# Cross-attention of a Perceiver layer: turns and products of one group issued between the steps of the next, reciprocal deviations turned by transposes

## The chip, the cores and the metric

The kernel runs on one core of one Trainium2 chip. The time is device microseconds from launch to end; three runs of the kernel before gave 571.45, 571.56 and 575.35 us, median 571.56 us. All arithmetic is in float32.

## What is computed

One layer: cross-attention of 32 x 32 queries on a context of 257 rows per batch entry, then self-attention with 16 heads, then a mixture of eight experts of which each token takes two. The change lies in the cross-attention alone:

```
def _L0_xattn_ref(modality1, modality2, ln1_g, ln1_b, ln2_g, ln2_b, Wq, bq, Wk, bk, Wv, bv, Wo, bo):
    x1 = layernorm(modality1, ln1_g, ln1_b)
    x2 = layernorm(modality2, ln2_g, ln2_b)
    q = x1 @ Wq + bq
    k = x2 @ Wk + bk
    v = x2 @ Wv + bv
    scores = jnp.einsum('bqe,bke->bqk', q, k) * scaling
    attn = jax.nn.softmax(scores, axis=-1)
    ctx = jnp.einsum('bqk,bke->bqe', attn, v)
    return ctx @ Wo + bo
...
x = x + _L0_xattn_ref(_layernorm(x, axis=-1), ctx_768, ...)
x = x + _L0_attn_ref(_layernorm(x, axis=-1), ...)
x = x + _L0_ffn_ref(_layernorm(x, axis=-1), ...)
```

x is (32, 32, 512), the context (32, 257, 384), every projection has 512 outputs.

## The kernel before

The 32 batch entries are taken in eight **groups** of four; a group has 4 x 32 = 128 query rows, one per partition. Two groups make a **pair**. Key and value projections are not carried out on the context: the kernel folds Wq with Wk (tile mq) and Wv with Wo (tile wvo) once, so that a group needs only products with the raw context, and the layernorm of the context comes in as one reciprocal standard deviation per context row.

For group g these steps exist, each a function:

- `cstats(g)` (L498): nine statistics instructions on VectorE over the context tile n and its last row nl, a few small ones, and on GpSimd the power -1/2 (L519), which gives rs, one number per context row, with context rows on the partitions. Its statistics are held behind an instruction in the table `pace`: those of group g+2 behind the instruction that makes u of group g (L597, L601).
- `rspread(g)` (L522): ScalarE repeats rs into rx (L526; one buffer only), four blocks of 32 equal columns, and copies the last row's number (L532).
- `xscores(g)` (L535): TensorE multiplies the queries q2T by the transposed context nT into pscore (L542). TensorE then turns rx into prs (L551) by an ordinary product with the identity, so that the deviations lie along the free dimension, and ScalarE copies it to rb (L555). VectorE multiplies pscore by rb and takes the row maximum (L558, then L565 and L567), ScalarE takes the exponential (L571), VectorE multiplies by rb again (L574): the tile ex.
- `xmix(g)` (L579): TensorE turns ex (two transposes into pte, L584), ScalarE copies it to eT (L586), TensorE multiplies eT by n into pc (L590), VectorE adds the last row and makes u (L597). It also issues the loads of group g+3, on SyncE's queue, and at g = 4 those of the four self-attention weights and the zero fill of a DRAM list.
- `xout(g)` (L611): TensorE turns u (three transposes into ptu, L615), ScalarE copies to uT (L617), TensorE multiplies by wvo into po (L620), VectorE adds to x_sb (L623).

For a pair p there are `xnorm(p)` (statistics of x and the normalised y), `xturn(p)` (eight transposes of y, L446, evacuated by ScalarE to x1T), `xquery(p)` (the queries: 36 products counted as instructions, L475, L467, L484) and `xbias(p)` (VectorE adds). `norm(0)`, `turn(0)` (L365), `project(0, j, half)` (L380, j = 0 for q and 1 for k) and `rotate(0, j)` (L396 to L409) belong to the self-attention stage and are already placed here for its first pair.

The loop (L726) writes, for each g: xscores(g), cstats(g+1), rspread(g+1), xout(g-1), then xturn or xquery of the next pair or a piece of the self-attention, and last xmix(g). The turn and its product stand side by side in xmix and in xout: on TensorE, pte, a wait for ScalarE's copy, pc; ptu, a wait for ScalarE's copy, po.

The program text is not the order on the engines. A scheduler of the framework lays out each engine's instructions before the run, keeps the text's order as priority, and by its own estimates of time lets later instructions go ahead of one that it takes to be waiting. On the engine the order is then fixed. PSUM tiles come from two pools of four buffers: `ps` (pscore, pc, po, pq, pb, pp, spt) and `ps2` (pte, prs, ptu, pt).

Of the kernel before, what the change touches and what calls it, by code (L numbers as in the profile page):

```python
# [28 lines left out]
NTT = 8  # L29
# [22 lines left out]
def tile_perceiver_layer(  # L52
# [22 lines left out]
    nc = tc.nc  # L75
# [16 lines left out]
    ident = cpool.tile([P, P], F32, name="ident")  # L92
# [132 lines left out]
    with ExitStack() as attn:  # L225
# [19 lines left out]
        with ExitStack() as xa:  # L245
# [246 lines left out]
            def xbias(p):  # L492
                for i in range(2):
                    nc.vector.tensor_add(
                        x_sb[:, 2 * p + i, :], x_sb[:, 2 * p + i, :], xrow
                    )

            def cstats(g):  # L498

                n, nl = gs[g]["n"], gs[g]["nl"]  # L500
                st = spool.tile([P, 9, 6], F32, tag="st9", bufs=2, name="st9")

                with tc.issue_after(pace["c", g]):
                    for r in range(9):
                        nc.vector.bn_stats(  # L505
                            st[:, r, :], n[:, r // 2, r % 2, :] if r < 8 else nl
                        )

                d = spool.tile([P, 9], F32, tag="d9", bufs=2, name="d9")
                nc.vector.tensor_tensor(d, st[:, :, 1], st[:, :, 4], ALU.subtract)  # L510
                nc.vector.scalar_tensor_tensor(
                    d, d, DC / 4.0, d, op0=ALU.mult, op1=ALU.mult
                )
                v = spool.tile([P, 9], F32, tag="v9", bufs=2, name="v9")
                nc.vector.tensor_tensor(v, st[:, :, 2], st[:, :, 5], ALU.add)
                nc.vector.tensor_tensor(v, v, d, ALU.add)
                nc.vector.tensor_scalar(v, v, 1.0 / DC, EPS, ALU.mult, ALU.add)  # L517
                rs = spool.tile([P, 9], F32, tag="rs9", bufs=2, name="rs9")
                nc.gpsimd.tensor_tensor(rs, v, mhalf[:, :9], ALU.pow)  # L519
                gs[g]["rs"] = rs  # L520
# [13 lines left out]

            def xscores(g):  # L535
                p, i = g // 2, g % 2
                q2T, qb, nT, rb = qs[p]["q2T"], qs[p]["qb"], gs[g]["nT"], gs[g]["rb"]
                pscore = ps.tile([P, D], F32, tag="ps", name="pscore")
                for c in range(KC):
                    for b in range(4):  # L540
                        o = i * P + b * T
                        nc.tensor.matmul(  # L542
                            pscore[ts(b, T), 0:S],
                            q2T[:, c, o : o + T],
                            nT[:, c, b, :],
                            start=(c == 0), stop=(c == KC - 1),
                        )

                pr = ps2.tile([P, 2, P], F32, tag="pt", name="prs")
                for c in range(2):  # L550
                    nc.tensor.matmul(  # L551
                        pr[:, c, :], gs[g]["rx"][:, c].rearrange("p b q -> p (b q)"),
                        ident, start=True, stop=True,
                    )
                nc.scalar.copy(rb[:, 0:NK], pr.rearrange("p c k -> p (c k)"))  # L555
                ex = wk.tile([P, S], F32, tag="ex", name="ex")
                mx = spool.tile([P, 1], F32, tag="mx", name="mx")
                top = nc.vector.tensor_tensor_reduce(  # L558
                    out=ex, in0=pscore[:, 0:S], in1=rb, scale=1.0, scalar=-3.0e38,
                    op0=ALU.mult, op1=ALU.max, accum_out=mx,  # L560
                )
                if g % 2 or g == 0:
                    pace["x", p + 1 + g % 2] = top.ins
                mq_ = spool.tile([P, 1], F32, tag="mq", name="mxq")
                nc.vector.tensor_tensor(mq_, mx, qb[:, i : i + 1], ALU.add)  # L565
                nm = spool.tile([P, 1], F32, tag="nm", name="nm")
                nc.vector.tensor_scalar(  # L567
                    nm, qb[:, i : i + 1], mq_, XSCALE, ALU.subtract, ALU.mult
                )
                sm = spool.tile([P, 1], F32, tag="sm", name="sm")  # L570
                gs[g]["exp"] = nc.scalar.activation(  # L571
                    ex, ex, AF.Exp, bias=nm, scale=XSCALE, accum_out=sm
                ).ins
                nc.vector.tensor_tensor(ex, ex, rb, ALU.mult)  # L574
                rc = spool.tile([P, 1], F32, tag="rc", name="rc")
                nc.vector.reciprocal(rc, sm)
                gs[g]["ex"], gs[g]["rc"] = ex, rc

            def xmix(g):  # L579

                n, nl, ex = gs[g]["n"], gs[g]["nl"], gs[g]["ex"]
                pt = ps2.tile([P, 2, P], F32, tag="pt", name="pte")
                for c in range(2):
                    nc.tensor.transpose(pt[:, c, :], ex[:, ts(c, P)], ident)  # L584
                eT = wk.tile([P, 2, P], F32, tag="eT", name="eT")
                nc.scalar.copy(eT, pt)  # L586
                pc = ps.tile([P, D], F32, tag="ps", name="pc")
                for c in range(2):
                    for b in range(4):
                        nc.tensor.matmul(  # L590
                            pc[ts(b, T), 0:DC],
                            eT[:, c, ts(b, T)],
                            n[:, b, c, :],
                            start=(c == 0), stop=(c == 1),
                        )
                u = wk.tile([P, DC], F32, tag="u", name="u")
                mixed = nc.vector.scalar_tensor_tensor(  # L597
                    u, nl, ex[:, NK : NK + 1], pc[:, 0:DC], op0=ALU.mult, op1=ALU.add
                )
                gs[g]["u"] = u  # L600
                pace["c", g + 2] = mixed.ins  # L601
                if g + 3 < NTT:
                    gs[g + 3] = load_ctx(g + 3)
                    if g + 4 == NTT:

                        with tc.issue_after(gs[g + 3]["last"]):
                            for n, s in zip("qkvo", (aWqT, aWkT, aWvT, aWoT)):
                                aw[n] = load_weight(s, weight_room("a" + n))
                        fill(aw["last"])

            def xout(g):  # L611
                u = gs[g]["u"]
                pt = ps2.tile([P, KC, P], F32, tag="pt", name="ptu")
                for c in range(KC):
                    nc.tensor.transpose(pt[:, c, :], u[:, ts(c, P)], ident)  # L615
                uT = wk.tile([P, KC, P], F32, tag="uT", name="uT")
                nc.scalar.copy(uT, pt)  # L617
                po = ps.tile([P, D], F32, tag="ps", name="po")
                for c in range(KC):
                    nc.tensor.matmul(  # L620
                        po, uT[:, c, :], wvo[:, c, :], start=(c == 0), stop=(c == KC - 1)
                    )
                nc.vector.scalar_tensor_tensor(  # L623
                    x_sb[:, g, :], po, gs[g]["rc"], x_sb[:, g, :],
                    op0=ALU.mult, op1=ALU.add,
                )
# [96 lines left out]
                nc.tensor.matmul(pm, firsts, part, start=True, stop=True)  # L723
                nc.vector.tensor_add(xrow, pm, row[:, RBO : RBO + D])

            for g in range(NTT):  # L726
                p = g // 2
                xscores(g)
                if g + 1 < NTT:
                    cstats(g + 1)  # L730
                    rspread(g + 1)
                if g == 0:
                    fold_values()
                    xbias(0)
                else:
                    xout(g - 1)
                if p + 1 < NTT // 2:
                    if g % 2 == 0:
                        if g == 0:
                            xnorm(1)  # L740
                        xturn(p + 1)
                        xbias(p + 1)
                    else:
                        xquery(p + 1)
                        if p + 2 < NTT // 2:
                            xnorm(p + 2)

                if g == NTT - 3:
                    norm(0)
                elif g == NTT - 2:  # L750
                    turn(0)
                elif g == NTT - 1:
                    project(0, 0, 1)
                    rotate(0, 0)
                xmix(g)
                if g >= NTT - 2:
                    project(0, g - (NTT - 2), 0)
            xout(NTT - 1)
            project(0, 1, 1)
            rotate(0, 1)  # L760

        av, ao = aw["v"], aw["o"]
# [776 lines left out]
```

## Time and profile before

| what | value |
|---|---|
| median of three runs | 571.56 us |
| the profiled execution, device time | 572.78 us |
| its span, first to last instruction | 571.0 us |
| mean granted TensorE clock | 0.975 |
| TensorE busy | 529.5 us (93%) |
| VectorE busy | 254.1 us (44%) |
| ScalarE busy | 123.5 us (22%) |
| GpSimd busy | 83.3 us (15%) |

The cross-attention's loop takes the stretch from 30.7 us (first pscore) to 146.6 us. Its groups start their score products (L542) at 30.67, 48.63, 63.51, 71.90, 87.70, 96.09, 111.31 and 123.37 us. In the lists of waits below, a line says which engine's instruction (tile and line) waited for which, then the microseconds in total, the number of waits, and the longest. In the timeline, a line has the start and the length in us, the engine, the line of the code, the operation, output <- inputs, the count, and in brackets the idle time before it with what ended it.

### The profile page before, as it was taken

Reading aid. Unit: us, or ns where it says so; the run is one execution under the profiler, and the core shown is the slowest. Engines: PE = TensorE matmul, PEld = TensorE weight load, DVE = VectorE, ACT = ScalarE, POOL = GpSimd, SP = SyncE. Lnnn points to the kernel's source line nnn. Section 1 sums busy time; section 2 is a strip of 40 time slices with the busy share of each in tenths; the row PEclk is TensorE's granted clock in tenths of the full one; section 3 lists DMA queues with packets and bytes.
Section 4 is the critical chain, followed back from the end, with each engine's and each line's share of the span. In section 5 each row is a group of like instructions: output and inputs, shape, how many; then the busy total and the mean of one; then the engine's idle time right before and its main releaser. Section 6 shows DMA issues by size and latency. Waiting matters only on the chain.

```text
span 571.0 us, 11331 instructions
## 1 busy us (share of the span) xinstructions
PE 529.5 (93%) x4732; PEld 344.2 (60%) x4732; DVE 254.1 (44%) x758; ACT 123.5 (22%) x274; POOL 83.3 (15%) x120
## 2 busy tenths in 40 slices
PE   6999887998999999998988999999999999999992
PEld 3655454655675685785647546556657475777580
DVE  6657688554677675577535122112213131222120
ACT  3533434231321412312113011001102020111010
POOL 2110231110000004004212110012120211112111
PEclk9999999999999989889889999999999999999997
DMA  7999967999920002002086323566553554746421
GB/s 275 382 366 381 350 215 260 361 385 386 386 95 38 2 3 113 4 2 115 34 332 265 116 42 137 188 178 212 160 137 111 161 199 153 210 161 194 158 26 21
DMA packets 43086, 104.51 MB, mean 183 GB/s; under 512 B 3985, under 2 KB 7185, under 8 KB 42002
## 3 DMA queue, kind: packets, MB, share of 16 engines
q1 hardware_dynamic: 38434, 94.91, 46.1%
q0 software_dynamic: 4592, 8.78, 7.4%
q8 instruction: 39, 0.64, 0.4%
q14 instruction: 21, 0.17, 0.1%
HBM read 75.50 MB, written 28.18 MB: 182 GB/s over the span
## 4 chain that ended last, share of the span: by engine, by line
PE 69%; DVE 2%; issue 1%; ACT 1%; POOL 0%; POOLq 0%; ACTq 0%
PE ph L1319 17%; PE fpo L1372 15%; PE pp L380 9%; PE ppv L793 5%; PE ppo L869 4%; PE fpq L1286 4%; PE phe L1123 2%; PE poe L1137 2%; PE pg L915 2%; PE pos L850 2%; PE pqs L808 2%; PE phb L1340 1%; PE xpt L1301 1%; ACT xT L176 1%; PE fpt L906 1%
## 5 line engine op out<-in xcount | busy, mean ns | idle before, releaser
L1319 PE MATMUL ph<-xT,w 128*128 128x288 f32 (+4 forms) x448 | 100.2, 382 | 3.1 <-ACT xT L176 3.1
L1319 PEld LDWEIGHTS ph<-xT,w 128*128 128x128 f32 x448 | 79.0, 190 | 19.6 <-ACT xT L176 3.7
L1372 PE MATMUL fpo<-w,hT 128*128 128x512 f32 x192 | 84.4, 596 | 0.0
L1372 PEld LDWEIGHTS fpo<-w,hT 128*128 128x128 f32 x192 | 35.9, 190 | 43.9 <-issue 43.7
L1325 DVE TENSOR_TENSOR hT<-ph,sg 128x288 f32<-128x288 f32 (+4 forms) x56 | 23.6, 422 | 63.3 <-ACT sg L1324 63.3
L1377 DVE TENSOR_SCALAR fob<-fpo,share 128x512 f32<-128x512 f32 x12 | 9.0, 751 | 77.0 <-PE fpo L1372 77.0
L1324 ACT ACTIVATE sg<-ph 128x288 f32<-128x288 f32 (+4 forms) x56 | 21.5, 384 | 85.0 <-PE ph L1319 85.0
L505 DVE BATCH_NORM_STATS2 st<-n 128x6 f32<-128x384 f32 x64 | 32.7, 548 | 2.0 <-DMA n<-in_ctx_dram 1.9
L194 POOL DMA_INDIRECT out_dram<-fob,idx x12 | 18.5, 1542 | 93.5 <-DVE fob L1377 80.9
L176 ACT COPY xT<-xpt 128x512 f32<-128x512 f32 (+2 forms) x12 | 6.0, 497 | 112.5 <-PE xpt L1301 112.4
L869 PE MATMUL ppo<-ao,oT 128*128 128x512 f32 x64 | 30.1, 624 | 0.0
L194 POOL DMA_INDIRECT out_dram<-fob,plc x9 | 13.9, 1541 | 101.7 <-DVE fob L1291 85.5
L620 PE MATMUL po<-wvo,uT 128*128 128x512 f32 x48 | 22.7, 610 | 3.9 <-ACT uT L617 3.8
L519 POOL TENSOR_TENSOR rs<-v,mhalf 128x9 f32<-128x9 f32 x8 | 14.4, 1799 | 77.3 <-DVE v L517 43.0
L380 PE MATMUL pp<-syT,aq 128*128 128x256 f32 x96 | 25.5, 425 | 0.0
L793 PE MATMUL ppv<-av,syT 128*128 128x512 f32 x48 | 23.2, 632 | 0.0
L475 PE MATMUL pq<-x1T,mq 128*128 128x256 f32 x96 | 22.4, 383 | 0.0
L1286 PE MATMUL fpq<-w,hT 128*32 128x128 f32 (+1 forms) x576 | 22.3, 309 | 0.0
L380 PE MATMUL pp<-syT,ak 128*128 128x256 f32 x96 | 22.3, 385 | 0.0
L1007 POOL DMA_INDIRECT xs_d<-fy,pi x16 | 17.0, 1063 | 34.9 <-DVE pi L1003 21.7
L380 PEld LDWEIGHTS pp<-syT,aq 128*128 128x128 f32 x96 | 20.1, 214 | 3.2
L869 PEld LDWEIGHTS ppo<-ao,oT 128*128 128x128 f32 x64 | 12.6, 199 | 14.2 <-issue 14.0
(269 smaller groups left out, 740.6 us busy)
## 6 DMA issues: line engine op xcount, KB each, us to landing
xs_d<-zero SPq DMA_DIRECT2D x8, 2112.0 KB, 20.4
w<-in_w1T_dram SPq DMA_DIRECT2D x16, 1024.0 KB, 6.6
w<-in_w2T_dram SPq DMA_DIRECT2D x16, 1024.0 KB, 7.3
nT<-in_ctxT_dram SPq DMA_DIRECT2D x8, 1542.0 KB, 8.0
n<-in_ctx_dram SPq DMA_DIRECT2D x32, 384.0 KB, 7.6
xs<-xs_d SPq DMA_DIRECT2D x4, 528.0 KB, 8.8
x_sb<-in_x_dram SPq DMA_DIRECT2D x8, 256.0 KB, 6.7
out_dram<-x_sb SPq DMA_DIRECT2D x8, 256.0 KB, 2.0
```

Source lines behind the costliest of these rows:

```text
L194: nc.gpsimd.indirect_dma_start(out=dst, out_offset=bass.IndirectOffsetOnAxis(ap=place, axis=0), in_=ob, in_offset=None, bounds_check=n * ( ...
L380: nc.tensor.matmul(pp[:, i, :], w[:, k, ts(e, P)], yT[:, k, :], start=(k == 0), stop=(k == KD - 1),)
L475: nc.tensor.matmul(pq[:, 0 : 2 * P], mq[:, k, ts(c, P)], x1T[:, k, :], start=(k == 0), stop=(k == KD - 1),)
L505: nc.vector.bn_stats(st[:, r, :], n[:, r // 2, r % 2, :] if r < 8 else nl)
L620: nc.tensor.matmul(po, uT[:, c, :], wvo[:, c, :], start=(c == 0), stop=(c == KC - 1))
L793: nc.tensor.matmul(pp, st[p]["yT"][:, k, ts(i, P)], av[:, k, :], start=(k == 0), stop=(k == KD - 1),)
L869: nc.tensor.matmul(pp, st[p]["oT", i][:, k].rearrange("p b q -> p (b q)"), ao[:, k, :], start=(k == 0), stop=(k == KD - 1),)
L1286: nc.tensor.matmul(po[ts(g, Q), 0:w], hT[:, f, ts(h, Q)], w2[:, f, ts(j, w)], start=(f == 0), stop=(f == KF - 1),)
L1319: nc.tensor.matmul(ph[:, 0:n], w1[:, k, ts(f, P)], t["xT"][:, k, 0:n], start=(k == 0), stop=(k == KD - 1),)
L1324: nc.scalar.activation(sg[:, 0:n], ph[:, 0:n], AF.Sigmoid)
L1325: nc.vector.tensor_mul(hT[:, f, 0:n], ph[:, 0:n], sg[:, 0:n])
L1372: nc.tensor.matmul(po, hT[:, f, ts(c, P)], w2[:, f, :], start=(f == 0), stop=(f == KF - 1),)
```

## The change

A wait on TensorE's side now has other work written between turn and product.

- `xscores(g)` keeps only the score product. The rest becomes `xweights(g)`.
- In `xweights` the turn of rx into prs is made of two transposes in place of two products with the identity.
- `xmix` is split into `xmix_turn` (pte and the copy to eT) and `xmix` (pc, u, the loads).
- `xout` is split into `xout_turn` (ptu and the copy to uT) and `xout` (po, x_sb).
- The loop has nine rounds. Round g: xmix_turn(g-1), xscores(g), xmix(g-1), xweights(g), cstats(g+1), rspread(g+1), xout_turn(g-1), xturn or xquery or turn(0) or project(0,0,0), xout(g-1). The ninth has project(0,1,0) and project(0,1,1) in the place of the scores and weights. xnorm(1) moves a few lines up.

```
@@ xscores
+                gs[g]["pscore"] = pscore
+
+            def xweights(g):
...
                 for c in range(2):
-                    nc.tensor.matmul(
-                        pr[:, c, :], gs[g]["rx"][:, c].rearrange("p b q -> p (b q)"),
-                        ident, start=True, stop=True,
+                    nc.tensor.transpose(
+                        pr[:, c, :], gs[g]["rx"][:, c].rearrange("p b q -> p (b q)"), ident
                     )
...
-            def xmix(g):
-
-                n, nl, ex = gs[g]["n"], gs[g]["nl"], gs[g]["ex"]
+            def xmix_turn(g):
+                ex = gs[g]["ex"]
...
                 nc.scalar.copy(eT, pt)
+                gs[g]["eT"] = eT
+
+            def xmix(g):
...
-            def xout(g):
+            def xout_turn(g):
...
                 nc.scalar.copy(uT, pt)
+                gs[g]["uT"] = uT
+
+            def xout(g):
+                uT = gs[g]["uT"]
...
-            for g in range(NTT):
+            for g in range(NTT + 1):
                 p = g // 2
-                xscores(g)
-                if g + 1 < NTT:
-                    cstats(g + 1)
-                    rspread(g + 1)
+                last = g == NTT
+                if g:
+                    xmix_turn(g - 1)
+                if last:
+                    project(0, 1, 0)
+                else:
+                    xscores(g)
+                if g:
+                    xmix(g - 1)
+                if last:
+                    project(0, 1, 1)
+                else:
+                    xweights(g)
+                    if g + 1 < NTT:
+                        cstats(g + 1)
+                        rspread(g + 1)
                 if g == 0:
                     fold_values()
                     xbias(0)
+                    xnorm(1)
                 else:
-                    xout(g - 1)
+                    xout_turn(g - 1)
                 if p + 1 < NTT // 2:
                     if g % 2 == 0:
-                        if g == 0:
-                            xnorm(1)
                         xturn(p + 1)
                         xbias(p + 1)
                     else:
...
                 elif g == NTT - 1:
+                    project(0, 0, 0)
+                if g:
+                    xout(g - 1)
+                if g == NTT - 1:
                     project(0, 0, 1)
                     rotate(0, 0)
-                xmix(g)
-                if g >= NTT - 2:
-                    project(0, g - (NTT - 2), 0)
-            xout(NTT - 1)
-            project(0, 1, 1)
             rotate(0, 1)
```

## The prediction

> **What bounds the kernel now.** I read the page first: shares, the 40 slices, the chain that ended last.
>
> ```profile
> PE 529.5 (93%) x4732; PEld 344.2 (60%) x4732; DVE 254.1 (44%) x758; ACT 123.5 (22%) x274; POOL 83.3 (15%) x120
> ...
> PE   6999887998999999998988999999999999999992
> ...
> DVE  6657688554677675577535122112213131222120
> ```
>
> TensorE is busy nearly everywhere. The chain of waits from 140 us to the end consists almost wholly of TensorE work, so a microsecond saved on TensorE before 146 us should reach the end. The low slices 4 to 6 and 8 to 9 are the cross-attention loop; VectorE is busiest there too. So I asked for the waits between 45 and 147 us:
>
> ```profile
> PE pc L590 <- ACT eT L586: 6.8, 7, 1.6
> ...
> PE po L620 <- ACT uT L617: 3.8, 6, 1.0
> ...
> PE prs L551 <- ACT rx L526: 1.0, 1, 1.0
> ...
> PE pb L484 <- ACT pbs L472: 0.2, 1, 0.2
> ```
>
> These four sum to 11.8 us. That is all that TensorE waits from the first pte (45.78) to the last project (146.49). The timeline of TensorE for the even round g = 2 and the start of the odd round 3 shows where they sit:
>
> ```profile
> 63.51 1.48 PE L542 MATMUL pscore<-nT,q2T 128*32 128x257 f32 x24
> 64.93 0.55 PE L615 MATMUL ptu<-ident,u 128*128 128x128 f32 x3
> 65.31 0.71 PE L446 MATMUL pt<-ident,y 128*128 128x128 f32 x5
> 66.04 2.84 PE L620 MATMUL po<-wvo,uT 128*128 128x512 f32 x6
> 68.72 0.49 PE L446 MATMUL pt<-ident,y 128*128 128x128 f32 x3
> 69.05 0.38 PE L584 MATMUL pte<-ident,ex 128*128 128x128 f32 x2
> 70.58 1.50 PE L590 MATMUL pc<-n,eT 128*32 128x384 f32 x16 [1.16 <-ACT eT L586]
> 71.90 1.48 PE L542 MATMUL pscore<-nT,q2T 128*32 128x257 f32 x24
> 73.31 0.71 PE L551 MATMUL prs<-ident,rx 128*128 128x128 f32 x4
> 73.86 0.49 PE L615 MATMUL ptu<-ident,u 128*128 128x128 f32 x3
> 74.92 2.84 PE L620 MATMUL po<-wvo,uT 128*128 128x512 f32 x6 [0.57 <-ACT uT L617]
> 77.60 3.62 PE L475 MATMUL pq<-x1T,mq 128*128 128x256 f32 x16
> ```
>
> The reader should see the pattern turn, gap, product; and that an even round is short (8.4 us from pscore to pscore), an odd one long (15.8, with the 6.3 us of xquery). From start to start the pieces cost: pscore 1.41, pc 1.31, prs 0.55, ptu 0.38, po 2.68, pte 0.26, xturn 0.96, xquery 6.32, one project 3.5 us.
>
> Last, the chain beside it, in the timeline of the other engines:
>
> ```profile
> 63.76 0.62 DVE L597 SCALAR_TENSOR_TENSOR u<-nl,ex,pc 128x384 f32<-128x384 f32 x1 [1.49 <-PE pc L590]
> ...
> 70.98 1.80 POOL L519 TENSOR_TENSOR rs<-v,mhalf 128x9 f32<-128x9 f32 x1 [11.38 <-DVE v L517]
> ...
> 72.81 0.41 ACT L526 COPY rx<-rs 128x256 f32<-128x256 f32 x1 [2.28 <-POOL rs L519]
> ```
>
> u of group 1 releases the statistics of group 3; rx of group 3 is done at 73.22, and prs needs it at 73.31. From u(1) to prs(3) is thus 9.55 us, and VectorE has no gap in the first 7.0 of it. This chain was just hidden; at g = 5 (87.97 to 98.53) it takes 10.6 and TensorE already waits 0.95 us for it.
>
> **What the Trainium skill says.** "Perfetto Trace Analysis", Optimizing Tensor Performance, Transposes: a logical transpose should use the transpose operation, not an ordinary product. The trace agrees: prs as product is four instructions of 275 ns, 0.55 us; pte, as many blocks as transposes, two of 273 ns, 0.26 us. The same page, Tensor Engine Instruction: TensorE's reported ends are estimated; hence I count from start to start. The same section: ScalarE, VectorE and GpSimd work strictly in order, only weight loads may pass ahead on TensorE. The trace agrees: at 58.97 rx(2) goes first on ScalarE after a 2.73 us wait for GpSimd, and a q2T copy, whose products ended near 57.4, follows only at 59.38.
>
> **The change part by part.**
>
> *Transposes for prs.* Groups 1 to 7: 7 x (0.55 - 0.26) = 2.0 us less on TensorE. Group 0 lies beside the start's other waits: nothing. Bounds 0 to 2.3.
>
> *pte, pscore, pc.* ScalarE's copy takes 0.37 us and pc started 0.9 to 2.5 us after pte. The 1.41 us of pscore now lie between. For the 1.60 us case (ScalarE was busy with y, norm(0) and q2T) nearly all is covered, since po now separates xquery from this place and q2T has 2.7 us more. The 6.8 us go; bounds 5.5 to 6.8.
>
> *ptu, filler, po.* Filler is xturn (0.96), turn(0) (0.88), xquery (6.3) or a project (3.5) against a need of about 0.7. Of the 3.8 us, 2.8 go. The last 0.97 stays: in round nine nothing is written between xout_turn(7) and xout(7).
>
> *Drain.* A piece followed by a gap costs about 0.11 us more than one followed by work (pte 0.38 against 0.26, ptu 0.49 against 0.38). With 13 gaps gone: 1.4 us.
>
> So far 6.8 + 3.8 + 1.0 + 0.2 of waits, 2.0 and 1.4: **15.2 us** gross. Against it stand new waits.
>
> *u.* ptu used to follow pc with pscore between (1.41 us); now only prs (0.26). In the trace ptu may start some 1.0 us after the last pc issues (u starts 0.25 after it, takes 0.62). Missing: 0.55. In odd rounds xquery, which takes another PSUM pool and whose x1T is long ready, can move ahead; in rounds 2 and 4 xturn takes its PSUM behind ptu and cannot, in round 6 turn(0) then leaves a similar gap before po. 3 x 0.55 = 1.7 us (bounds 0 to 4).
>
> *The deviations.* In an even round TensorE has between u(g-1) and prs(g+1): prs 0.26, ptu 0.38, the gap 0.55, xturn 0.96, po 2.68, pte 0.26, pscore 1.41, pc 1.31 = 7.8 us. The chain over VectorE, GpSimd and rx has kept its 9.5 (g = 3) to 10.6 (g = 5): waits 1.7 and 2.8. For g = 7 the chain is 10.4 (111.57 to 122.0), and project(0,0,0), which stood before pscore(7), now comes after prs(7); TensorE has about 7.4 us: wait 3.0. Together 7.5, if nothing moves ahead. xquery and project may go ahead of prs as far as the scheduler sees the wait; but it sees GpSimd's 1.8 us as short (rx(2) was placed ahead of a copy that could have run 1.5 us sooner), so I let it fill 0.1 + 1.2 + 1.4 = 2.7. 4.8 us remain (bounds 0 to 7.5).
>
> *The rest.* Last uT 1.0, pb and queueing on ScalarE 0.7.
>
> *At no cost.* Loads on SyncE's queue stay behind pc: group g+3's n landed 7.6 us (median) after issue, and is wanted two u's later; even rounds do not get shorter than that chain, so it stays hidden, by a microsecond or two. The aq load (issued 101.99, 7.2 us to landing) is wanted later in the text than before; 119.7 leaves 10 us. The fill (to 147 us on SyncE) only shifts. Buffers: pscore, pc and two pq fill the four of `ps`; the third needs pscore free, 3.6 us after xquery began, enough for rb and L558.
>
> Sum: 15.2 - (1.7 + 4.8 + 1.0 + 0.7 = 8.2) = **7.0 us**. The profiled execution took 572.78 us (span 571.0), 1.2 above the median; off the span 7.0 leaves 564.0, off the median **564.6 us**.
>
> **The rivals.**
>
> *Everything is filled* (0.17): the scheduler hides the deviations' chain and u with xquery and project. 15.2 less the last uT and slack, 2.2, is 13: 558.6. For: odd rounds have much independent work. Against: GpSimd's time, and VectorE at 83 and 94% of the even rounds (6.98 of 8.39, 7.87 of 8.39).
>
> *The other engines swallow it* (0.24): the even round is VectorE's and GpSimd's, nothing is filled (2.7 more) and 1 to 2 us of queueing come on top: gain 3, 568.6. For: g = 5 waits for rx already.
>
> *Slower* (0.06): ScalarE, in order, gets rx(g+1) ahead of exp(g) in the even rounds. exp then waits for GpSimd: ex at about 10.3 us after u(g-1), then pte, pscore, pc: 13.3 us per even round in place of 8.4, 3 x 4.9 = 14.7 lost, less about 8.7 gained in the odd rounds and at the start: 577.6. It decides once an even round grows by more than 2.9 us. For: rx stood ahead of q2T. Against: exp is ready 4 us before the scheduler can think rx ready.
>
> *It doesn't do what it says*: the scheduler already moved prs ahead of pc at 46.00, so part of the new order could exist before; but nothing filled the thirteen gaps, so it isn't the same order.
>
> **How the numbers follow.** The forecast itself gets 0.53, about 562 to 567. Under 565.8 (1%, about what a measurement tells from no change) lie the first rival and three quarters of the forecast: 0.17 + 0.40 = 0.57. Over 577.3 lies the slower case, with a little for the unforeseen, 0.07. Within 1%: 0.36. The range drops the slower case and the edge of the filled one: 558 to 571.
>
> **What would show it.** Right: waits pc <- eT near 0, po <- uT about 1 in one wait, prs x2 at 0.26, new waits prs <- rx of 1 to 3 us at g = 3, 5 and 7. Wrong: pte waiting for ex, pscore for q2T, statistics waiting for DMA, or a stage after 147 us that grows.

## The result and the profile after

The changed kernel takes 566.83 us (median of 8 runs), the kernel before 571.76 us in the same comparison; the ratio is 0.9892, with a 95% interval of 0.9864 to 0.992. The forecast was 564.6 us, 7.0 less than before. The medians are 4.9 us apart; the ratio, taken on the time before, comes to 6.2 us (4.6 to 7.8 by its interval).

The page of the changed kernel, engines' shares and slices:

```profile
PE 525.1 (93%) x4716; PEld 340.8 (60%) x4716; DVE 254.0 (45%) x758; ACT 123.2 (22%) x274; POOL 83.5 (15%) x120
...
PE   6999797999999999998969999999999999999992
...
DVE  6657778747567765668534032203122121222220
```

The span is 564.5 us against 571.0. To see the loop alone I measure on TensorE from the first pmv (L710 before, L723 after) to the first pgm, which follows the last project: 32.44 to 146.49 = 114.05 us before, 30.82 to 139.69 = 108.87 after. The **loop** is 5.2 us shorter. What follows it has not changed (424.5 before, 424.8 after). The remaining 1.6 us lie ahead of the loop, and ahead of pmt too, an early product that starts at 19.80 us against 21.46; from there to pmv it takes 11.0 us in both. The start of pmt varied from 19.7 to 22.0 us over all these runs. So "the loop" is the sharper measure, and I give it beside each time. It comes from one trace of each kernel; how much it varies from run to run is not known, and a few tenths are not read as an effect.

The waits of TensorE in the changed kernel, 40 to 143 us (who waited for which; us, times, longest):

```profile
PE prs L557 <- ACT rx L526: 4.3, 3, 1.9
...
PE ptu L624 <- DVE u L606: 2.1, 2, 1.7
PE pc L599 <- ACT eT L590: 1.9, 2, 1.7
...
PE po L633 <- ACT uT L626: 1.2, 2, 1.0
```

They sum to 9.5 us, where there were 11.8. The gaps after the turns did fall, from 6.8 + 3.8 to 3.1 us. But the waits for the deviations and for u, 1.0 us before, are now 6.4. The other 2.9 us of the loop's 5.2 are less work: 2.0 of shorter prs (seven times 0.28), and by difference 0.9, which I put down to drains. Rounds 2 and 3, in TensorE's timeline:

```profile
63.00 1.04 PE L446 MATMUL pt<-ident,y 128*128 128x128 f32 x8
63.87 2.74 PE L633 MATMUL po<-wvo,uT 128*128 128x512 f32 x6
66.45 0.38 PE L588 MATMUL pte<-ident,ex 128*128 128x128 f32 x2
66.76 1.51 PE L542 MATMUL pscore<-nT,q2T 128*32 128x257 f32 x24
68.08 1.47 PE L599 MATMUL pc<-n,eT 128*32 128x384 f32 x16
71.44 0.44 PE L557 MATMUL prs<-ident,rx 128*128 128x128 f32 x2 [1.88 <-ACT rx L526]
71.72 1.03 PE L475 MATMUL pq<-x1T,mq 128*128 128x256 f32 x4
```

pte, pscore, pc now run without a gap, and TensorE comes to prs(3) 1.88 us before rx is there. From u(1), at 61.94, to prs(3) at 71.44 it is 9.5 us, as it was before the change. The two pairs in the middle did not get shorter at all: from pscore(2) to pscore(4) and on to pscore(6) it took 24.19 and 23.61 us before, and takes 24.13 and 23.71 now (57.20, 81.33, 105.04). In each of the two the waits grew by 0.6 us (from 3.3 to 3.9 and from 2.7 to 3.3), and the shorter work gave it back. What was gained lies ahead of them and behind them.

### The profile page after: what moved, and what is told of

It is laid out like the page before. It is cut to its first block, busy times and chain, and to the rows that moved or that the text cites. A ratio compares the mean times of both kernels' runs of the same rounds, so it can differ in the third digit from the quotient of the medians.

```text
span 564.5 us, 11301 instructions
## 1 busy us (share of the span) xinstructions
PE 525.1 (93%) x4716; PEld 340.8 (60%) x4716; DVE 254.0 (45%) x758; ACT 123.2 (22%) x274; POOL 83.5 (15%) x120
## 4 chain that ended last, share of the span: by engine, by line
PE 69%; DVE 2%; issue 1%; ACT 1%; POOL 0%; POOLq 0%; ACTq 0%
PE ph L1344 18%; PE fpo L1397 15%; PE pp L380 8%; PE ppv L818 5%; PE ppo L894 4%; PE fpq L1311 4%; PE phe L1148 3%; PE poe L1162 2%; PE pg L940 2%; PE pos L875 2%; PE pqs L833 2%; PE phb L1365 1%; PE xpt L1326 1%; ACT xT L176 1%; PE fpt L931 1%
## 5 line engine op out<-in xcount | busy, mean ns | idle before, releaser
L519 POOL TENSOR_TENSOR rs<-v,mhalf 128x9 f32<-128x9 f32 x8 | 14.4, 1798 | 80.7 <-DVE v L517 42.6
```

## The experiments

In the comparisons below the kernel before had medians of 572.7 to 573.0 us, about 1 us above the one in the result, so the ratios say more than the times.

**The two parts apart: the order alone, the transposes alone.**

```
# order_alone: the changed kernel, in xweights
-                    nc.tensor.transpose(pr[:, c, :], rx..., ident)
+                    nc.tensor.matmul(pr[:, c, :], rx..., ident, start=True, stop=True)
# transposes_alone: the kernel before, in xscores: the same lines the other way round
```

> The changed kernel with prs made by two products with the identity again; the order of the steps stays changed. My theory: behind the new order nothing hides prs any more (pc stands before it, ptu after it), so each of seven groups pays 0.28 us more: about 2.0 us above the changed kernel, near 568.8, still some 3 us under the kernel before. Rival, the transposes carry the whole gain: no better than before, 571.7. Rival, prs lies hidden in the waits for rx: same as the changed kernel, 566.8.

> The kernel before with prs made by transposes and nothing else changed. My theory: in the old order prs of groups 1, 2, 4 and 6 stands in the gap in which pc waits for eT, so what it saves becomes wait; only groups 3, 5 and 7 bring 0.28 us each, with group 0 about 1 us: near 570.8. Rival, every transposed prs pays in full as in the prediction's 2.0: 569.7.

Measured: order_alone 566.99 us, ratio to before 0.9906 (0.9872 to 0.9939), loop 108.62. That is the second rival: beside the new order the transposes bring nothing that these runs show. What they save on TensorE comes back as wait; order_alone waits 7.4 us where the changed kernel waits 9.5:

```profile
PE prs L557 <- ACT rx L526: 4.5, 3, 1.9
PE pc L600 <- ACT eT L591: 1.4, 2, 0.7
PE po L634 <- ACT uT L627: 1.0, 1, 1.0
PE ptu L625 <- DVE u L607: 0.5, 1, 0.5
```

transposes_alone: 571.03 us, ratio 0.9968 (0.995 to 0.9986), loop 112.61, 1.4 shorter than before. In the loop my theory stood for 0.8 us (three times 0.28; group 0 lies ahead of it) and the rival for 2.0, so this lies in the middle and decides for neither. In the old order the transposes do bring something.

**The two turns apart.**

```
# eT_split_only: the changed kernel
-                    xout_turn(g - 1)          # ahead of xturn / xquery
...
                 if g:
+                    xout_turn(g - 1)
                     xout(g - 1)
# uT_split_only: the changed kernel
-                    xmix_turn(g - 1)          # ahead of xscores
...
                 if g:
+                    xmix_turn(g - 1)
                     xmix(g - 1)
```

> The changed kernel with xout_turn put back directly before xout, so that only the turn of ex has a step between it and its product. My theory: the waits po <- uT come back in part (the scheduler may put pte between ptu and po), 1.5 to 3 us, so 568 to 570. Rival, the gain comes from the turn of ex alone: 566.8.

> The changed kernel with xmix_turn put back directly before xmix (after the scores), so that only the turn of u has other work between it and its product. My theory: the waits pc <- eT come back, about 5 us, less what prs fills of them: 569.5 to 571. Rival, the turn of u brings the gain: 566.8 to 567.5.

Measured: eT_split_only 571.39 us, ratio 0.9988 (0.9971 to 1.0005), loop 113.41; uT_split_only 569.12, ratio 0.994 (0.992 to 0.996), loop 112.09. The first is a miss: I expected 568 to 570, and it is no faster than the kernel before that can be told. Its waits say most of why:

```profile
PE po L633 <- ACT uT L626: 6.1, 7, 1.9
PE prs L557 <- ACT rx L526: 3.4, 3, 1.3
PE ptu L624 <- DVE u L606: 1.5, 1, 1.5
PE pte L588 <- DVE rc L581: 0.5, 1, 0.5
```

The scheduler put pte between ptu and po in odd rounds and nothing in even ones, and the wait that had gone at eT stands at uT, 6.1 us where the kernel before has 3.8. In uT_split_only the waits for eT came back with 4.9 us, as expected. One split brings 0.6 us of loop, the other 2.0, both together 5.2, each with the transposes, which alone bring 1.4. With one gap left open, the waits come to 11.5 and 11.3 us, hardly less than the 11.8 before.

eT_split_only has one thing more, in round 4. The po of round 3 takes 2.84 us; that of round 4, after two waits close together, takes 4.25:

```profile
78.84 2.84 PE L633 MATMUL po<-wvo,uT 128*128 128x512 f32 x6 [0.35 <-ACT uT L626]
...
87.13 0.55 PE L624 MATMUL ptu<-ident,u 128*128 128x128 f32 x3 [1.48 <-DVE u L606]
89.58 4.25 PE L633 MATMUL po<-wvo,uT 128*128 128x512 f32 x6 [1.91 <-ACT uT L626]
```

From 89.6 to 94.2 us TensorE's granted clock was 0.64; over the whole loop it is 1.00 in the kernel before and in the changed one. From that po to the next pscore it took 4.6 us, in the changed kernel 2.9, so some 1.7 us of this loop are a slower TensorE. Without them the turn of ex alone would bring about 2.3 us of loop, an estimate. Whether the other runs of this kernel have this stretch too is not known.

**What holds the even rounds: the power on GpSimd taken away, and doubled.**

```
# recip_dve: the changed kernel, in cstats
-                nc.gpsimd.tensor_tensor(rs, v, mhalf[:, :9], ALU.pow)
+                nc.vector.reciprocal(rs, v)
# pool_twice: the changed kernel, in cstats
                 nc.gpsimd.tensor_tensor(rs, v, mhalf[:, :9], ALU.pow)
+                nc.gpsimd.tensor_tensor(rs, rs, mhalf[:, :9], ALU.pow)
```

> The changed kernel with the context rows' power -1/2 on GpSimd (1.8 us a group) left out and a reciprocal on VectorE in its place; only the values of the deviations differ. My theory: the chain from u(g-1) to rx(g+1) sets the even rounds, so the waits prs <- rx (4.3 us) and the ScalarE copies that queue behind rx shrink; the loop from the first pmv to pgm, 108.9 us in the changed kernel, comes to 104 to 106, the time 3 to 5 us under the changed kernel: 562 to 564. Rival: VectorE sets the even rounds, the waits move to u and eT, and the loop stays within 1 us of 108.9.

> The changed kernel with the power on the context rows' deviations taken twice on GpSimd, one after the other; only the values of the deviations differ. My theory: each of the three even-round chains (rx of groups 3, 5, 7) grows by 1.8 us and TensorE waits for all of it, and rx of the others delays what queues on ScalarE: loop 108.9 + 5 to 8, time 572 to 575, about what the kernel before takes. Rival, VectorE sets the rounds: loop less than 3 us longer.

Measured: recip_dve 560.21 us, ratio to before 0.9787 (0.9761 to 0.9813), loop 102.23: 6.6 us shorter than the changed kernel's, more than I expected. (recip_dve leaves out the power -1/2 and pool_twice takes it twice, so neither computes the layer; they tell of the loop's time alone.) The waits for rx and eT are all but gone, and with them the rival that VectorE sets these rounds, for it has one instruction more in each:

```profile
PE ptu L624 <- DVE u L606: 1.7, 2, 1.3
PE po L633 <- ACT uT L626: 1.2, 2, 1.0
PE prs L557 <- ACT rx L526: 0.2, 1, 0.2
PE pc L599 <- ACT eT L590: 0.2, 1, 0.2
```

pool_twice: loop 124.74 us, 15.9 longer than the changed kernel's, where I expected 5 to 8. (Its time of 965.28 us says nothing on this: it makes 1024 expert products ph in place of 448, presumably because other deviations send the tokens elsewhere.) Its waits from 33 to 160 us:

```profile
PE prs L558 <- ACT rx L527: 10.2, 3, 3.7
PE pc L600 <- ACT eT L591: 5.6, 2, 3.6
PE ptu L625 <- DVE u L607: 1.7, 1, 1.7
PE po L634 <- ACT uT L627: 1.2, 2, 1.0
```

These are 18.7 us, 9.2 more than in the changed kernel. The other 6 or so are a slower TensorE after the longest waits, of which below. Two more things are seen here. The order of TensorE's instructions through the loop is the same in the two programs, though a power of 1.8 us was added to the chain: the scheduler did not answer to that time. (In recip_dve it did move one prs, that of group 4, ahead of pc; how it reckons is not shown.) And waits for eT grew although nothing on their own path changed: the copy to eT stands behind rx on ScalarE.

That queue is also where the changed kernel's 1.67 us at pc(1) comes from. ScalarE's timeline of the changed kernel; pte(1) had been issued at 56.88:

```profile
57.65 0.40 ACT L526 COPY rx<-rs 128x256 f32<-128x256 f32 x1 [3.12 <-POOL rs L519]
57.96 0.19 ACT L532 COPY rb<-rs 128x1 f32<-128x1 f32 x1
58.55 1.52 ACT L432 ACTIVATE y<-x_sb,nb,rs 128x512 f32<-128x512 f32 x2 [0.40 <-ACT rb L532]
59.98 0.35 ACT L590 COPY eT<-pte 128x256 f32<-128x256 f32 x1
```

The reader should see three instructions in a row that each need a number from GpSimd (L519, then L425), and the copy that TensorE waits for behind them.

**The transposes once more, with the chain short.**

```
# recip_products: recip_dve, with prs by two products as in order_alone
```

> recip_dve (a reciprocal on VectorE in the place of GpSimd's power; only the values of the deviations differ) with prs made by two products with the identity again. My theory: in the changed kernel the transposes brought nothing because TensorE waited for rx and u anyhow; with that chain short, TensorE sets the pace and the longer prs pays: loop 102.2 + 1.5 to 2.0. Rival: prs stays hidden for another reason, loop 102.2.

Measured: 563.35 us, ratio to before 0.984 (0.9816 to 0.9864), loop 103.47, which is 1.24 us more than recip_dve. The scheduler also moved some of the query products by a few places between the two. It is somewhat under the 1.5 to 2.0 expected, but not nothing: with the chain short, prs pays; in the changed kernel, which waits for rx and u, it doesn't.

**Work ahead of prs.** Where the scheduler leaves TensorE waiting for rx, the text can put independent products.

```
# fill_ahead: the changed kernel, in the loop, ahead of xweights(g)
+                    ahead = {3: 1, 5: 2}.get(g, 0)
+                    if ahead:
+                        xquery(p + 1, range(ahead))
+                    elif g == NTT - 1:
+                        project(0, 0, 0)
                     xweights(g)
...
-                        xquery(p + 1)
+                        xquery(p + 1, range(ahead, KC))
# fill_last: besides, in the last round
-                    project(0, 1, 1)
+                    project(0, 1, 1, (0,))
...
+                if last:
+                    project(0, 1, 1, (1,))
                 if g:
                     xout(g - 1)
```

> The changed kernel with independent products written ahead of prs: in round 3 the first of the three query blocks, in round 5 the first two, in round 7 all of project(0,0,0). My theory: the waits prs <- rx fall from 4.3 to about 1.5 us because TensorE works through them; the loop gets 2 to 3 us shorter (about 106.5). Rival: the order on TensorE does not matter while VectorE, GpSimd and ScalarE set the pace; the products only leave a hole elsewhere (pte <- ex, po <- uT), and the loop stays at 108.9.

> As fill_ahead, and in the last round the second half of project(0,1,1) stands between xout_turn(7) and xout(7). My theory: the last wait po <- uT of 0.97 us goes as well, nothing replaces it: 0.5 to 1.0 us under fill_ahead. Rival: the split product makes ptu wait for u instead, no gain.

Measured: fill_ahead 561.55 us, ratio to before 0.9819 (0.9783 to 0.9855), loop 104.92, 4.0 us under the changed kernel's, more than the 2 to 3 expected. TensorE's waits in it, without a line for rx:

```profile
PE po L637 <- ACT uT L630: 2.2, 3, 1.0
PE ptu L628 <- DVE u L610: 1.8, 2, 1.5
PE pc L603 <- ACT eT L594: 1.7, 1, 1.7
```

fill_last: 562.82 us, ratio 0.984 (0.9812 to 0.9868), loop 104.19. The loop is 0.7 us shorter, as expected; the time doesn't tell the two apart.

**y, xbias and norm(0) held back.**

```
# held_after: the changed kernel; held: the same on fill_last
+                        with tc.issue_after(pace["e", g - 1]):   # the copy to eT
+                            xnorm_y(p + 1)                       # y, from xnorm
...
+                            with tc.issue_after(pace["c", g + 1]):   # u of g - 1
                                 xbias(p + 1)
...
+                    with tc.issue_after(pace["c", g + 1]):
                         norm(0)
```

> As fill_last; besides, the normalisation of the queries (y, 1.5 us on ScalarE) is held behind the copy to eT, and xbias and norm(0) on VectorE behind u. My theory: the remaining waits pc <- eT (1.7, group 1) and ptu <- u (1.5, round 4) come from ScalarE and VectorE standing in order on work that itself waits for GpSimd; both go, the loop of fill_last (104.2 us) falls to 101 to 102.5, the time 1.5 to 3 us under fill_last. Rival: the held work comes late for xturn and rx, and the loop stays at 104 or grows.

> The same holding of y, xbias and norm(0) on the changed kernel, without the products written ahead. My theory: the waits for eT and u (1.9 and 2.1 us) fall to 0.5 each, but TensorE then meets prs <- rx sooner, which grows by a part of it: loop 106 to 108 against 108.9. Rival: the chain to rx absorbs all of it, loop 108.9.

Measured: held_after 562.52 us, ratio 0.9811 (0.9788 to 0.9833), loop 105.37, so 3.5 us shorter than the changed kernel's, a little more than expected: eT's waits went altogether, u's fell to 1.0, rx's to 3.8. Not all of it is the holding: in round 3 the scheduler now put a query block ahead of prs, where it put nothing in the changed kernel, much as fill_ahead does by hand; the two shares are not told apart. held: 562.99, ratio 0.9835 (0.9813 to 0.9857), loop 104.29, no better than fill_last: the rival. One wait prs <- rx of 1.4 us is back, in round 3: on VectorE the xbias held back now stands, from 65.5 to 67.0 us, ahead of v, from which GpSimd makes rs. It comes with 1.1 us in three waits for u and 0.7 for eT. The two kernels with the reciprocal and pool_twice aside, fill_ahead and held_after are the fastest measured, both clear of the kernel before and with intervals below the changed kernel's; between them and fill_last or held these runs don't decide.

## Why the prediction was right, and where it was off

The direction and the exchange hold: the gaps behind the turns closed, and new waits for rx, of about the size forecast, took part of the gain back. 566.83 is 2.2 us above the forecast and within its range. Of the 7.0 us the loop gave 5.2; the 1.6 us ahead of it stood in no term. By its steps:

- *pte, pscore, pc.* "The 6.8 us go; bounds 5.5 to 6.8." 4.9 went. **This is the term that was most mis-sized.** The step took the long wait for a matter of q2T and y in one round and did not follow ScalarE's queue behind GpSimd: at pc(1) y and rx stand ahead of the copy, 1.67 us. In held_after, where y is held back, that wait is gone. Of the 1.9 us that stayed, the sum had allowed 0.7 as queueing.
- *ptu, filler, po.* 2.8 of 3.8 were to go; 2.6 went. The last 0.97 stayed, as said.
- *Transposes.* 2.0 us of work were to go, and 2.0 went. In the sum of work and waits the term holds. But it is not what the transposes are worth in this order: order_alone goes without them, has 2.1 us less of waits, and its loop is no longer. The work saved was handed to waits that stand a few steps on, above all those for u (2.1 us against 0.5). A part of this was in the prediction's sum: its waits for u were worked out with prs at 0.26, and with 0.55 each of the three would have been 0.29 shorter. The other 1.1 us were booked as gain, and order_alone shows none of them.
- *Drain.* 1.4 forecast, for 13 gaps gone; some 0.9 by the loop's sum. The new waits are gaps as well: there were 15 before and there are 9 now, so 6 went, which at 0.11 us each is 0.7.
- *u.* 1.7 us forecast, 2.1 found, but not for the reason given. In round 2 it was 0.37, and in round 6 0.25 at po; in round 4 it was 1.70, because xbias and norm(0), waiting for y and GpSimd, stood ahead of u on VectorE (pc had begun at 83.06):

```profile
84.12 1.26 DVE L494 TENSOR_TENSOR x_sb<-x_sb,xrow 128x512 f32<-128x512 f32 x2
...
85.35 0.69 DVE L354 TENSOR_TENSOR x_sb<-x_sb,row 128x512 f32<-128x512 f32 x1
...
85.96 0.61 DVE L606 SCALAR_TENSOR_TENSOR u<-nl,ex,pc 128x384 f32<-128x384 f32 x1
...
86.62 0.55 PE L624 MATMUL ptu<-ident,u 128*128 128x128 f32 x3 [1.70 <-DVE u L606]
```

- *The deviations.* 4.8 us forecast in three waits at g = 3, 5 and 7; 4.3 found, as 1.88, 1.39 and 1.03. The scheduler put nothing ahead of prs(3), one query block of four products ahead of prs(5) and five of the eight products of project(0,0,0) ahead of prs(7), much as guessed. This term was right in mechanism and nearly in size; recip_dve and pool_twice show that this chain, and not VectorE's load, holds the even rounds.
- *The rest.* Loads and fill stayed hidden: TensorE waits for no DMA in the loop.

The differences close the sum: pc 1.2 (after the 0.7 of queueing), po 0.2, drains 0.5, u 0.4, less 0.5 for the deviations, together 1.8 us of the 7.0.

That the total came so near is in part luck. By the prediction's own terms about 2.8 us should have come in rounds 2 to 5: 6.0 us of waits, 1.2 of prs and 0.7 of drains, against 4.3 of new waits and 0.7 of queueing. Nothing came there: the waits for rx were as forecast (3.3 us against 3.2), but eT and u took 4.0 us where 1.8 were allowed, and no drains went, for there are as many gaps as before. The rounds ahead and behind gave 5.2 us where 4.2 were left to them.

Of the rivals, "everything is filled", with a gain of 13 us, came nearer once the products were written ahead of prs (the loop of fill_ahead is 9.1 us under that of the kernel before). "Slower", with rx ahead of exp on ScalarE, did not happen; its relation, rx and y ahead of eT, did, at 1.67 us.

## What to carry to other kernels

When a gap on the busy engine is filled, look for the chain that was just hidden beside it: here 9.5 us from u to prs, which had 0.1 us to spare, and which no filling of gaps could shorten. Then either shorten it (without the GpSimd instruction of 1.8 us in each group the loop was 6.6 us shorter, though the layer needs that power) or put independent work where the engine will come too early, by hand where the scheduler leaves the wait open (4.0 us here). Follow each in-order queue for what stands behind an instruction that waits: the copy that TensorE needs may be ready to run and third in line.

## What was not expected of the hardware

In pool_twice a long wait cost more than itself. TensorE's timeline and the windows with its granted clock (busy times of the engines, then PEclk, DMA share, GB/s):

```profile
64.78 2.71 PE L600 MATMUL pc<-n,eT 128*32 128x384 f32 x16 [3.57 <-ACT eT L591]
...
93.87 1.50 PE L600 MATMUL pc<-n,eT 128*32 128x384 f32 x16 [2.08 <-ACT eT L591]
```

```profile
64.70:69.00 4.30, 4.12 (x25) 1.66 (x26) 1.95 (x6) 0.57 (x3) 0.00 (x0) 0.60 0.21 63
69.00:73.00 4.00, 4.00 (x27) 2.15 (x28) 4.00 (x12) 3.06 (x8) 0.00 (x0) 1.00 1.00 340
```

After a wait of 3.57 us the same pc took 2.71 us, at a granted clock of 0.60 over the next 4.3 us; after one of 2.08 us it took 1.50. Waits of 3.73, 3.24 and 3.25 us had the same effect, each with some 1.5 us of slower work, at clocks of 0.62 to 0.72. Over four such waits that is about 6 us, what the waits alone left unexplained. The Trainium skill, "TensorE: Matmul & The Clock Gate", HAM oscillation, says that idle gaps over about 3.4 us lower TensorE's clock; here 3.24 us was enough, and less can be. In eT_split_only, shown above, waits of 1.48 and 1.91 us with one short ptu between them did the same; in pool_twice waits of 2.08 and 1.69 us, 1.9 us of work apart, did not. So the length of a single wait doesn't settle it, and how idle time is weighed these runs don't show. In the changed kernel's loop no wait is longer than 1.9 us, and the granted clock is 1.00.
